# Batch sizes, output loads and the order of the last groups in a graph layer's sum over edges

## The chip, the core and the metric

The kernel runs on one core of a Trainium2 chip. The time is device microseconds (us) of one execution, the median of several; before the change it is 1443.45 us (three runs, 1440.51 to 1446.14). A core has TensorE (PE, matmuls; its weight loads are listed as PEld), VectorE (DVE), ScalarE (ACT), GpSimd (POOL), and SyncE (SP), which issues plain DMAs. POOL issues the indirect DMAs, the gathers.

## What is computed

One layer of a graph network on 12,500 nodes of 128 features, with 200,000 edges sorted by destination and four edge types. Cut to what matters:

```python
h = jnp.maximum(_layernorm(x, axis=-1), 0.0)
xs = h[src]
for i in range(4):
    msgs = msgs + jnp.where((edge_type == i)[:, None], xs @ W[i] + b[i], 0.0)
out = x + jax.ops.segment_sum(msgs, dst, num_segments=N)
```

Destinations are drawn as the square of a uniform number, so low node numbers get far more edges than high ones.

## The kernel before

Edges are cut into 1563 chunks of 128. The normalised features are kept in a table `htab` in HBM as three bf16 parts of each number (384 columns a node). There are two ways to sum the edges of a node.

*Gathered chunks.* The 1083 chunks from number 480 on are taken in groups of 16 (66 full groups, then groups of 12, 8, 4 and 3). For a chunk, `gather` (L440) fetches 128 rows of the table with one indirect DMA into half of a group's tile `hm`; a tile holds 8 chunks and there are five such tiles. VectorE makes a one-hot matrix `oh` from the destination and type of each edge (L461), TensorE multiplies the gathered rows by it (L498, three matmuls a chunk, one for each part), ScalarE copies the sums `ps` to `sb` (L505), TensorE applies the bias (L510) and the four weight matrices (L512) into `py`, and VectorE adds 16 windows of `py` into a ring buffer at rows that it reads from `brow` (`add_up`, L515 and L524). The first eight groups ("raw") gather `x` itself and normalise it, since the table is still being built. Raw groups put their additions on a list `waiting`, which the next group empties.

When the ring has a node block that no later chunk reaches, `put_out` and `leave` write it: load the rows of `x` into `xo` (L538), transpose the sums on TensorE (L546), add on VectorE (L549), store (L551, L553). A list `flushes` holds the blocks, with a due chunk for each (L577), and `goes` names the group after which each is written; what is not due among the full groups leaves after the last group.

*Counted nodes.* The first 480 chunks go to 1224 destinations with many edges each. For those the kernel counts how often each table row and type occurs. `count` takes a batch of nodes: for each slot (up to 128 edges of a node) VectorE makes two one-hot matrices `o` (L782 or L786, and L787), TensorE multiplies them (L791), and ScalarE copies the result to `counts` as 8-bit numbers (L794), two nodes in one 16-bit number where they can share. The two `o` tiles hold four slots each. `multiply` then reads the whole table once for a batch, 25 loads `hs` of up to 384 KB (L823, five buffers), with three matmuls for each of 98 table blocks (L826, 294 in all), whose moving columns are four times the batch's nodes; then a product with the weights (L841) and additions into `acc`. `dense_work` runs the multiplication of one batch beside the counting of the next.

There are 1260 entries (a node with very many edges has several), in batches of 22, 46, twelve of 92, 42 and 46. The first two take only nodes that share a slot; later ones mix in nodes that have several slots.

What sets the order: Python emits the work of a group, and `pace` says how far the dense work should be after each part of a group, counted in matmul columns; from the last full group on, all that is left is emitted. The blocks `tc.issue_after(mm)` tie the emitted work to a matmul; the framework then orders each engine's instructions. The engines run them in that order and wait for one another by semaphores. SP's loads stand in one queue, POOL's gathers in another.

```python
ends_in = [12, 8, 4, 3]
sizes = [G] * FULL + ([r] if r else []) + ends_in
```

`check_all` (L591) checks the ring's ranges and the counts, and sets a flag; the program's last part runs a slow version if the flag is set.

Of the kernel before, what the change touches and what calls it, by code (L numbers as in the profile page):

```python
# [48 lines left out]
P = 128  # L49
# [3 lines left out]
SG = 4  # L53
WIN = 32
RAW = 8
ROOM = 12
C0 = 480
VBMAX = 92
MANY = 16
# [3 lines left out]
OT = 4  # L63
# [6 lines left out]
def kernel(  # L70
# [56 lines left out]
    shared = [(0, d) for d in range(PAIRS, ND)]  # L127

    VB = VBMAX
    sizes_of = [VB // 8 * 2, VB // 4 * 2]  # L130
    left = len(alone) + len(shared) - sum(sizes_of) - VB // 4 * 2
    sizes_of += [VB] * (left // VB) + ([left % VB] if left % VB else []) + [VB // 4 * 2]
    batches = []
    a = b0 = 0
    for i, n in enumerate(sizes_of):

        na, ns = len(alone) - a, len(shared) - b0
        n1 = 0 if i < 2 else min(round(n * na / (na + ns) / 2) * 2, na)
        n1 = max(n1, n - ns)
        batches.append(alone[a : a + n1] + shared[b0 : b0 + n - n1])  # L140
        a, b0 = a + n1, b0 + n - n1
# [309 lines left out]
    def sum_up(t0, g, rows, raw, last):  # L451
        win = window_of(C0 + t0)
        K = NT * win
        if raw:
            oh = npool.tile([P, G, P], F32, name="ohf")[:, :, :K]
        else:
            while waiting:
                waiting.pop()()
            oh = opool.tile([P, G, P], BF16, name="oh")[:, :, :K]
        for i in range(g):  # L460
            nc.vector.tensor_scalar(  # L461
                oh[:, i, :], (iota_f if raw else iota_b)[:, :K], keyf[:, t0 + i : t0 + i + 1], None, ALU.is_equal
            )
        if raw:
            for h0 in range(0, g, HG):
                row = lambda k: rows(h0 + k, 0, 1)
                n = min(HG, g - h0)
                of = stats(row, n, P, npool, "")
                normalize(row, row, n, P, of)

            with tc.issue_after(of[2]):
                while waiting:
                    waiting.pop()()
        sb = spool.tile([P, G * P], F32, name="sb")[:, : G * K].rearrange("p (g t n) -> p g t n", g=G, t=NT)
        def types():

            ohv = oh.rearrange("p g (t n) -> p g t n", t=NT)
            pc = s_ps.tile([R, G * WIN], F32, name="ps")[:, : G * win].rearrange("p (g n) -> p g n", g=G)
            for t in range(NT):
                if raw:  # L480
                    nc.tensor.matmul(pc[:, :g, :], pick_f[:, t, :], ohv[:, :g, t, :], start=(t == 0), stop=(t == NT - 1))  # L481
                else:
                    nc.tensor.matmul(  # L483
                        pc[t * CG : (t + 1) * CG, :g, :], three, ohv[:, :g, t, :], start=True, stop=True, tile_position=(0, t * CG)
                    )
            cnt = spool.tile([R, G * WIN], BF16, name="cnt")[:, : G * win].rearrange("p (g n) -> p g n", g=G)
            nc.scalar.copy(cnt[:, :g], pc[:, :g])  # L487
            return cnt

        R = N3 if raw else P  # L490
        cnt = None if raw else types()
        nparts = 1 if raw else 3
        for i0 in range(0, g, SG):
            i1 = min(i0 + SG, g)
            ps = s_ps.tile([P, SG, P], F32, name="ps")[:, :, :K]
            for i in range(i0, i1):
                for c in range(nparts):
                    mm = nc.tensor.matmul(  # L498
                        ps[:, i - i0, :],
                        rows(i, c, nparts),  # L500
                        oh[:, i, :],
                        start=(c == 0),
                        stop=(c == nparts - 1),
                    )
            nc.scalar.copy(sb[:, i0:i1].rearrange("p g t n -> p g (t n)"), ps[:, : i1 - i0, :])  # L505
            yield i1 / g, mm.ins
        if raw:
            cnt = types()
        py = (x_ps.tile([P, G * WIN], F32, name="pt") if last else y_ps.tile([P, G * WIN], F32, name="py"))[:, : G * win].rearrange("p (g n) -> p g n", g=G)
        nc.tensor.matmul(py[:, :g, :], b12 if raw else b128, cnt[:, :g, :], start=True, stop=False)  # L510
        for t in range(NT):
            mm = nc.tensor.matmul(py[:, :g, :], wsb[:, t, :], sb[:, :g, t, :], start=False, stop=(t == NT - 1))  # L512

        def add_up():
            _, at = nc.values_load_multi_w_load_instructions(  # L515
                brow[0:1, t0 : t0 + g],
                engines=[DVE],
                min_val=0,
                max_val=RING - 1,
                skip_runtime_bounds_check_because="the row is clamped to this range on the chip",  # L520
            )
            for i in range(g):
                to = ring[:, bass.ds(at[i], win)]
                nc.vector.tensor_tensor(to, to, py[:, i, :], ALU.add)  # L524

        if raw:
            waiting.append(add_up)
        else:
            add_up()
        yield 1, mm.ins  # L530


    def leave(j0, j1, of, c0):

        nf = min(j1, N // P) - j0
        xt = outp.tile([P, OT, D], F32, name="xo")
        if nf:
            nc.sync.dma_start(xt[:, :nf, :], x[j0 * P : (j0 + nf) * P, :].rearrange("(j p) d -> p j d", p=P))  # L538
        if j0 + nf < j1:
            r = rows_of(j1 - 1)  # L540
            nc.sync.dma_start(xt[:r, nf, :], x[(j1 - 1) * P :, :])
        pt = x_ps.tile([P, OT, DO], F32, name="pt")
        for j in range(j0, j1):
            r = rows_of(j)
            k = c0 + (j - j0) * P
            nc.tensor.transpose(pt[:r, j - j0, :], of[:, k : k + r], ident)  # L546
        for r, a0, a1 in ((P, 0, nf), (rows_of(j1 - 1), nf, j1 - j0)):
            if a1 > a0:
                nc.vector.tensor_add(xt[:r, a0:a1, :], pt[:r, a0:a1, :], xt[:r, a0:a1, :])  # L549
        if nf:  # L550
            nc.sync.dma_start(out[j0 * P : (j0 + nf) * P, :].rearrange("(j p) d -> p j d", p=P), xt[:, :nf, :])  # L551
        if j0 + nf < j1:
            nc.sync.dma_start(out[(j1 - 1) * P :, :], xt[: rows_of(j1 - 1), nf, :])  # L553
# [18 lines left out]
    while flushes[-1][1] < NW:  # L572
# [1 line left out]
        jb = min(ja + OT, NW, (ja * P // RING + 1) * RING // P)  # L574
        flushes.append((ja, jb, 0))
    assert NDT * P <= RING - 512
    flushes = [(ja, jb, T * (min(jb * P, N) / N) ** 0.5 + ROOM - C0) for ja, jb, _ in flushes]  # L577


    ends_in = [12, 8, 4, 3]  # L580
# [2 lines left out]
    sizes = [G] * FULL + ([r] if r else []) + ends_in  # L583
    starts = [sum(sizes[:i]) for i in range(len(sizes))]

    goes = [
        next((i for i in range(RAW, FULL) if starts[i] + sizes[i] >= c), len(sizes) - 1) for _, _, c in flushes
    ]


    def check_all():  # L591

        low = const.tile([P, BM], F32, name="low")
        step = const.tile([P, BM], F32, name="step")
# [1 line left out]
        for (ja, jb, _), i in zip(flushes, goes):  # L596
            if starts[i] + sizes[i] < TM:
# [1 line left out]
                    step, rowf, starts[i] + sizes[i] - 0.5, (jb - ja) * float(P), ALU.is_gt, ALU.mult  # L599
                )  # L600
                nc.vector.tensor_add(low, low, step)
        bad = const.tile([P, 5], F32, name="bad")
        hi = const.tile([P, 4], F32, name="hi")
        nc.vector.tensor_sub(low, head, low)
        nc.vector.tensor_reduce(hi[:, 0:1], ends[:, :, 0], AX.X, ALU.max)
# [3 lines left out]
        nc.vector.tensor_single_scalar(bad[:, 0:1], hi[:, 0:1], -0.5, op=ALU.is_gt)  # L609
        nc.vector.tensor_single_scalar(bad[:, 1:3], hi[:, 1:3], -0.5, op=ALU.is_lt)  # L610
        nc.vector.tensor_single_scalar(bad[:, 3:4], hi[:, 3:4], RING - WIN + 0.5, op=ALU.is_gt)
        nc.vector.tensor_single_scalar(bad[:, 4:5], most, MANY + 0.5, op=ALU.is_gt)
        many = const.tile([P, 3], F32, name="many")
        nc.vector.tensor_reduce(many[:, 0:1], bad, AX.X, ALU.add)
# [301 lines left out]
    for gi, (t0, g) in enumerate(zip(starts, sizes)):  # L916
# [71 lines left out]
                prep_edges(q, q + 1, later, 1)  # L988
        if gi == RAW - 1:
            assert done >= len(tables)  # L990
        for part, mm in sum_up(t0, g, rows, raw, gi >= FULL):

            with tc.issue_after(mm):
                while work and spent < pace(gi, part):
                    spent = next(work, None)
                    if spent is None:
                        work = None
        if gi in SLOT_STEPS:
            with tc.issue_after(mm):
                for _ in range(SLOT_STEPS[gi]):  # L1000
                    next(to_slots, None)
        if gi == RAW - 1:
# [4 lines left out]
            whats.close()  # L1007
            outp = mid.enter_context(tc.tile_pool(name="outp", bufs=3))
            later = mid.enter_context(tc.tile_pool(name="later", bufs=1))
            dense = mid.enter_context(tc.tile_pool(name="dense", bufs=2))  # L1010
            sdp = mid.enter_context(tc.tile_pool(name="sdp", bufs=1))
            ohp = mid.enter_context(tc.tile_pool(name="ohp", bufs=2))
            hsp = mid.enter_context(tc.tile_pool(name="hsp", bufs=5))
            work = dense_work()
        for (ja, jb, _), i in zip(flushes, goes):
            if i == gi:
                put_out(ja, jb, t0 + g < TM)
        if work is None and not dense_out and gi > RAW:
            dense_out = True
            assert goes[0] < gi  # L1020
            for ja in range(0, NDT, OT):
                leave(ja, min(ja + OT, NDT), acc, ja * P)
        if dense_out and not checked:
            checked = True
            check_all()
# [126 lines left out]
```

## Time and profile before

| what | value |
|---|---|
| median of three runs | 1443.45 us |
| the profiled execution's own time | 1440.69 us |
| its span, first to last instruction | 1439.0 us |
| mean granted TensorE clock | 0.937 |
| raw groups, table building and slots | about 0 to 219 us |
| first gather from `htab` to the end of the last | 177.2 to 1414.9 us |
| matmuls of L826 | 4704, 715.7 us busy |
| HBM traffic of all DMAs | 290.10 MB |

In the profile's rows "out<-in" are the program's tile names. A mean of one instruction is from its start to its end; matmuls overlap, so the step from one to the next is shorter than that. In brackets stands how long the engine was idle before an instruction and what ended the idle time. The chain of waits follows the work that ended last back in time. "Built order" below means the order of instructions on each engine in the compiled program, which holds no times.

### The profile page before, as it was taken

The numbers are of one execution on the slowest core, as the hardware profiler recorded it, in microseconds if no ns is written. First come the engines' busy times: TensorE is split into PE (matmuls) and PEld (weight loads), VectorE is DVE, ScalarE is ACT, GpSimd is POOL, SyncE is SP. The second block draws the span as 40 slices with busy tenths as digits, with TensorE's granted clock in tenths as the row PEclk, the third lists the DMA queues.
The fourth block names the chain that finished last, engine by engine and source line by source line (L and its number), as shares of the span: only waits on it lengthen the run. The fifth ranks groups of instructions, "written<-read, shape, count | busy, mean of one in ns | idle before, by whom it ended". The sixth has DMA issues, their size and how long they took to land.

```text
span 1439.0 us, 31409 instructions
## 1 busy us (share of the span) xinstructions
PE 1274.2 (89%) x10210; PEld 857.0 (60%) x10210; DVE 982.2 (68%) x5310; ACT 598.0 (42%) x1922; POOL 1059.0 (74%) x1093
## 2 busy tenths in 40 slices
PE   0656687989999899999999997899999999999975
PEld 0434455765666566666656664566666666668763
DVE  8698696888888667657575765586676766557323
ACT  7776445352343535243343534244343535233220
POOL 7777777575777777777777777777777777777772
PEclk9765678999999999999999998899999999999997
DMA  6543247965666576776667674667667676768952
GB/s 210 176 153 104 93 150 255 312 214 168 201 197 201 173 238 193 233 221 203 212 200 221 208 223 139 193 203 216 210 206 223 195 210 206 220 207 288 324 184 82
DMA packets 144633, 290.10 MB, mean 202 GB/s; under 512 B 27116, under 2 KB 74654, under 8 KB 144462
## 3 DMA queue, kind: packets, MB, share of 16 engines
q1 hardware_dynamic: 94526, 185.71, 39.9%
q0 software_dynamic: 49936, 102.34, 24.7%
q8 instruction: 80, 1.31, 0.4%
q14 instruction: 91, 0.75, 0.2%
HBM read 271.91 MB, written 16.03 MB: 200 GB/s over the span
## 4 chain that ended last, share of the span: by engine, by line
PE 67%; DVE 8%; DMA 6%; POOL 6%; issue 3%; ACT 3%; DVEq 0%; SPq 0%; ACTq 0%; POOLq 0%
PE pa L826 36%; PE pt L791 10%; PE py L512 8%; PE ps L498 7%; POOL hm L440 6%; DMA hs<-htab 3%; ACT counts L794 2%; DVE ring L524 2%; DVE o L787 2%; DMA hm<-htab,srcT 1%; DVE o L786 1%; DVE oh L461 1%; PE ps L481 1%; PE py L841 1%; PE ps L483 1%
## 5 line engine op out<-in xcount | busy, mean ns | idle before, releaser
L440 POOL DMA_INDIRECT hm<-htab,srcT x955 | 925.2, 969 | 313.5 <-issue 267.5
L826 PE MATMUL pa<-counts,hs 128*128 128x368 fp8e4 (+3 forms) x4704 | 715.7, 298 | 14.4 <-DMA hs<-htab 13.1
L826 PEld LDWEIGHTS <-hs 128*128 128x128 bf16 x4704 | 427.8, 98 | 239.1 <-DMA hs<-htab 20.2
L794 ACT ACTIVATE counts<-pt 128x392 uint16<-128x392 f32 x630 | 309.4, 504 | 279.1 <-PE pt L791 275.7
L787 DVE TENSOR_SCALAR o<-iota_n,hkT 128x392 bf16<-128x392 f16 x1083 | 359.5, 332 | 0.0
L791 PE MATMUL pt<-o,o 128*128 128x392 bf16 x1083 | 278.9, 334 | 6.6 <-ACT counts L794 2.5
L524 DVE TENSOR_TENSOR ring<-ring,py 128x16 f32 (+4 forms) x1056 | 182.2, 173 | 124.3 <-PE py L512 104.0
L461 DVE TENSOR_SCALAR oh<-iota_b,keyT 128x64 bf16<-128x64 bf16 (+4 forms) x955 | 174.0, 264 | 107.3 <-PE ps L498 106.6
L505 ACT COPY sb<-ps 128x256 f32<-128x256 f32 (+5 forms) x271 | 111.8, 417 | 311.8 <-PE ps L498 276.7
L498 PE MATMUL ps<-oh,hm 128*128 128x64 bf16 (+4 forms) x2865 | 154.3, 202 | 29.5 <-DMA hm<-htab,srcT 29.1
L498 PEld LDWEIGHTS <-hm 128*128 128x128 bf16 x2865 | 131.5, 99 | 64.2 <-DMA hm<-htab,srcT 36.0
L512 PE MATMUL py<-sb,wsb 128*128 128x384 f32 (+4 forms) x528 | 164.5, 452 | 0.0
L440 POOL DMA_INDIRECT hm<-in_x_dram,srcT x128 | 132.3, 1033 | 41.8 <-issue 36.0
L782 DVE TENSOR_SCALAR o<-iota_b,loT 128x128 bf16<-128x128 bf16 x375 | 99.1, 264 | 88.5 <-PE pt L791 87.8
L786 DVE TENSOR_SCALAR o<-iota_b,loT,byT 128x128 bf16<-128x128 bf16 x333 | 110.9, 333 | 40.6 <-PE pt L791 40.1
L791 PEld LDWEIGHTS <-o 128*128 128x128 bf16 x1083 | 100.4, 99 | 56.3 <-DVE o L787 10.9
L794 ACT ACTIVATION_READ_ACCUMULATOR counts<-pt 128x1 f32 x630 | 131.9, 209 | 0.0
L512 PEld LDWEIGHTS py<-sb,wsb 128*128 128x128 f32 x528 | 105.8, 211 | 35.2 <-issue 9.9
L498 PE MATMUL ps<-ohf,hm 128*128 128x48 f32 x256 | 59.1, 385 | 52.9 <-ACT hm L402 52.9
L487 ACT CAST cnt<-ps 128x256 bf16<-128x256 f32 (+7 forms) x70 | 28.6, 409 | 165.5 <-PE ps L483 144.9
L786 DVE TENSOR_SCALAR o<-iota_b,loT 128x128 bf16<-128x128 bf16 x375 | 95.9, 256 | 1.3 <-PE pt L791 1.2
L498 PEld LDWEIGHTS ps<-ohf,hm 128*128 128x128 f32 x256 | 52.1, 291 | 71.7 <-ACT hm L402 59.1
(188 smaller groups left out, 641.9 us busy)
## 6 DMA issues: line engine op xcount, KB each, us to landing
hs<-htab SPq DMA_DIRECT2D x384, 384.0 KB
hm<-htab,srcT POOLq DMA_INDIRECT x955
htab<-h SPq DMA_DIRECT2D x11, 768.0 KB
xo<-in_x_dram SPq DMA_DIRECT2D x23, 256.0 KB
out_dram<-xo SPq DMA_DIRECT2D x23, 256.0 KB
xt<-in_x_dram SPq DMA_DIRECT2D x6, 512.0 KB
hs<-htab SPq DMA_DIRECT2D x16, 192.0 KB
xt<-in_x_dram SPq DMA_DIRECT2D x5, 448.0 KB
```

Of the source, the lines that this page charges most:

```text
L440: nc.gpsimd.indirect_dma_start(out=rows[:, (i - h0) * width : (i - h0 + 1) * width], out_offset=None, in_=table, in_offset=bass.IndirectOf ...
L461: nc.vector.tensor_scalar(oh[:, i, :], (iota_f if raw else iota_b)[:, :K], keyf[:, t0 + i : t0 + i + 1], None, ALU.is_equal)
L498: mm = nc.tensor.matmul(ps[:, i - i0, :], rows(i, c, nparts), oh[:, i, :], start=(c == 0), stop=(c == nparts - 1),)
L505: nc.scalar.copy(sb[:, i0:i1].rearrange("p g t n -> p g (t n)"), ps[:, : i1 - i0, :])
L512: mm = nc.tensor.matmul(py[:, :g, :], wsb[:, t, :], sb[:, :g, t, :], start=False, stop=(t == NT - 1))
L524: nc.vector.tensor_tensor(to, to, py[:, i, :], ALU.add)
L782: nc.vector.tensor_scalar(o1[:, k, :], iota_b, loT[:, s : s + 1], None, ALU.is_equal)
L786: nc.vector.tensor_scalar(o1[:, k, :], iota_b, loT[:, s : s + 1], by, ALU.is_equal, ALU.mult)
L787: nc.vector.tensor_scalar(o2[:, k, :], iota_n, hkT[:, s : s + 1], None, ALU.is_equal)
L791: nc.tensor.matmul(pb, o1[:, k, :], o2[:, k, :], start=first, stop=last)
L794: nc.scalar.activation(counts[:, :, i * NT : (i + 1) * NT], pb.rearrange("p (b t) -> p b t", t=NT), AF.Copy, accum_out=both[:, i : i + 1],)
L826: nc.tensor.matmul(pa[:, : nv * NT], hs[:, j - j0, c * D : (c + 1) * D], counts[:, j, : nv * NT], start=(j == 0 and c == 0), stop=(j == NW ...
```

## The change

There are five edits.

1. Batches: the batch that isn't full (1260 entries less 13 x 92, so 64) comes first, and all others have 92, so that 14 batches are left of 16. Only the first takes shared nodes alone.
2. Counting buffers are given back once the dense work is done. In their room a pool `outs` holds all outputs that are still to come, and their rows of `x` are loaded there at once (`fetch`); `leave` uses them.
3. Due times: the margin is no longer 12 chunks but 2 plus 6 standard deviations of the number of edges, in chunks. A block may now leave after the last group but one. Three of the 24 blocks leave one group earlier by this, among them the last but one (from node 92 x 128 on), which leaves after the group of 4.
4. In the small groups at the end, all of a group's instructions are tied to the matmuls of the group before it (`behind`), so that matmuls stand in group order. The last group's additions wait until the block that leaves ahead of it has been written.
5. `check_all` is split: the range checks run at group 63.

```diff
-ROOM = 12
+ROOM = 6
...
-    sizes_of = [VB // 8 * 2, VB // 4 * 2]
-    left = len(alone) + len(shared) - sum(sizes_of) - VB // 4 * 2
-    sizes_of += [VB] * (left // VB) + ([left % VB] if left % VB else []) + [VB // 4 * 2]
+    left = len(alone) + len(shared)
+    sizes_of = ([left % VB] if left % VB else []) + [VB] * (left // VB)
...
-        n1 = 0 if i < 2 else min(round(n * na / (na + ns) / 2) * 2, na)
+        n1 = 0 if i < 1 else min(round(n * na / (na + ns) / 2) * 2, na)
...
-        if raw:
+        if raw or t0 + g == TM:
             waiting.append(add_up)
...
+    def due(jb):
+
+        q = (min(jb * P, N) / N) ** 0.5
+        return T * q + 2 + ROOM * (q * (1 - q) * E) ** 0.5 / P - C0
...
+        next((i for i in [*range(RAW, FULL), final - 1] if starts[i] + sizes[i] >= c), final) for _, _, c in flushes
...
+        behind = ExitStack()
+        if gi >= FULL:
+            behind.enter_context(tc.issue_after(mm))
         for part, mm in sum_up(t0, g, rows, raw, gi >= FULL):
...
+        behind.close()
...
+            counting.close()
+            leaves = [(ja, min(ja + OT, NDT)) for ja in range(0, NDT, OT)]
+            late = [(ja, jb) for (ja, jb, _), i in zip(flushes, goes) if i >= gi]
+            outp = mid.enter_context(tc.tile_pool(name="outs", bufs=len(leaves + late)))
+            for ja, jb in leaves + late:
+                seen_out[ja] = fetch(ja, jb)
+            for ja, jb in leaves:
+                leave(ja, jb, acc, ja * P)
+        for (ja, jb, _), i in zip(flushes, goes):
+            if i == gi < final - 1:
+                put_out(ja, jb, True)
+        if gi == final:
+
+            for ahead in (True, False):
+                for (ja, jb, _), i in zip(flushes, goes):
+                    if i >= final - 1 and (i < final) == ahead:
+                        put_out(ja, jb, False)
+                while waiting:
+                    waiting.pop()()
+        if gi == FULL - 3:
+            assert q == BM - 1
+            check_chunks()
```

`fetch` is the part of `leave` that loads `x`, made a function of its own.

More of the change, by code (lines that the diff above doesn't have):

```diff
@@ L530, in sum_up, with fetch @@
         yield 1, mm.ins
-    def leave(j0, j1, of, c0):
+    seen_out = {}
+    def fetch(j0, j1):
         nf = min(j1, N // P) - j0
@@ L541, in leave @@
             nc.sync.dma_start(xt[:r, nf, :], x[(j1 - 1) * P :, :])
+        return xt
+    def leave(j0, j1, of, c0):
+        nf = min(j1, N // P) - j0
+        xt = seen_out.pop(j0) if j0 in seen_out else fetch(j0, j1)
         pt = x_ps.tile([P, OT, DO], F32, name="pt")
@@ L576 @@
     assert NDT * P <= RING - 512
-    flushes = [(ja, jb, T * (min(jb * P, N) / N) ** 0.5 + ROOM - C0) for ja, jb, _ in flushes]
+    def due(jb):
+        q = (min(jb * P, N) / N) ** 0.5
+        return T * q + 2 + ROOM * (q * (1 - q) * E) ** 0.5 / P - C0
+    flushes = [(ja, jb, due(jb)) for ja, jb, _ in flushes]
     ends_in = [12, 8, 4, 3]
@@ L584, with check_chunks @@
     starts = [sum(sizes[:i]) for i in range(len(sizes))]
+    final = len(sizes) - 1
     goes = [
-        next((i for i in range(RAW, FULL) if starts[i] + sizes[i] >= c), len(sizes) - 1) for _, _, c in flushes
+        next((i for i in [*range(RAW, FULL), final - 1] if starts[i] + sizes[i] >= c), final) for _, _, c in flushes
     ]
-    def check_all():
+    bad = const.tile([P, 5], F32, name="bad")
+    def check_chunks():
         low = const.tile([P, BM], F32, name="low")
@@ L601, in check_all @@
                 nc.vector.tensor_add(low, low, step)
-        bad = const.tile([P, 5], F32, name="bad")
         hi = const.tile([P, 4], F32, name="hi")
@@ L611, in check_all @@
         nc.vector.tensor_single_scalar(bad[:, 3:4], hi[:, 3:4], RING - WIN + 0.5, op=ALU.is_gt)
+    def check_all():
         nc.vector.tensor_single_scalar(bad[:, 4:5], most, MANY + 0.5, op=ALU.is_gt)
@@ L1009 @@
             later = mid.enter_context(tc.tile_pool(name="later", bufs=1))
[L1010 to L1013, printed above, removed]
+            counting = mid.enter_context(ExitStack())
+            dense = counting.enter_context(tc.tile_pool(name="dense", bufs=2))
+            sdp = counting.enter_context(tc.tile_pool(name="sdp", bufs=1))
+            ohp = counting.enter_context(tc.tile_pool(name="ohp", bufs=2))
+            hsp = counting.enter_context(tc.tile_pool(name="hsp", bufs=5))
             work = dense_work()
-        for (ja, jb, _), i in zip(flushes, goes):
-            if i == gi:
-                put_out(ja, jb, t0 + g < TM)
         if work is None and not dense_out and gi > RAW:
@@ L1020 @@
             assert goes[0] < gi
-            for ja in range(0, NDT, OT):
-                leave(ja, min(ja + OT, NDT), acc, ja * P)
+            counting.close()
[19 more added lines that the diff above has]
+            check_chunks()
         if dense_out and not checked:
```

## The prediction

> **What bounds the kernel now.** The page comes first, because its shares mislead here: TensorE looks like the limit.
>
> ```profile
> span 1439.0 us, 31409 instructions
> PE 1274.2 (89%) x10210; PEld 857.0 (60%) x10210; DVE 982.2 (68%) x5310; ACT 598.0 (42%) x1922; POOL 1059.0 (74%) x1093
> L440 POOL DMA_INDIRECT hm<-htab,srcT x955 | 925.2, 969 | 313.5 <-issue 267.5
> ```
>
> The POOL row says otherwise. One gather takes 969 ns and 0.30 us passes before the next, so 955 of them need 955 x 1.27 = 1212 us if nothing stops them. The gathers run from 177.2 to 1414.9, which is 1237.6 us. So POOL is stopped for only about 24 us; all the rest is back to back. POOL's timeline, filtered to the long gaps, shows where:
>
> ```profile
> 280.08 0.94 POOL L440 DMA_INDIRECT hm<-htab,srcT  x1 [10.85 <-PE ps L498]
> 332.32 0.94 POOL L440 DMA_INDIRECT hm<-htab,srcT  x1 [8.72 <-PE ps L498]
> ```
>
> Five tiles hm of 8 gathers each exist, so POOL waits there for the matmuls of L498 five tiles earlier. From 332 to 1414.9 there are only two more gaps (2.2 and 0.6 us, at 966 and 987). **The time is therefore: start of gathers (177.2) + 1212 + 24 of stops + what follows the last gather (1414.9 to 1439.0, 24.1 us).** A change helps only through the stops, through slower gathers, or behind the last one.
>
> Why is TensorE late at 280? Its chain of waits in 219 to 345 names the table loads:
>
> ```profile
> 231.74 6.59 DMA hs<-htab
> 239.06 6.34 DMA hs<-htab
> 245.44 0.65 PE pa L826 x12
> 246.12 5.52 DMA hs<-htab
> 255.24 7.04 DMA hs<-htab
> ```
>
> The first batch has 22 nodes. Its 12 matmuls per load take about half a microsecond, while a 384 KB load arrives every 1.2 us: the batch is bound by DMA (share 0.84, 291 GB/s in 219.5 to 262). Between 219.5 and 280, 41 us of matmul steps take 60.
>
> **The change, part by part.** *Batches.* Sixteen batches (22, 46, twelve of 92, 42, 46) become fourteen (64 and thirteen of 92); nodes, columns and the 1083 counted slots stay. Two passes over the table go: 2 x 294 matmuls, 50 loads, 19 MB of 290. What are 588 small matmuls worth? By the rows, from first start to last end, less one matmul's own length:
>
> ```profile
> 249.49 0.65 PE L826 MATMUL pa<-counts,hs 128*128 128x88 fp8e4 x12 [0.54 <-DMA hs<-htab]
> 1299.81 1.90 PE L826 MATMUL pa<-counts,hs 128*128 128x168 fp8e4 x24
> 260.39 1.11 PE L826 MATMUL pa<-counts,hs 128*128 128x184 fp8e4 x12
> 499.70 1.41 PE L826 MATMUL pa<-counts,hs 128*128 128x368 fp8e4 x8
> ```
>
> (0.65-0.21)/11 = 40 ns for 88 columns, 72 for 168, 79 for 184, 156 for 368: 0.42 ns a column and no fixed part. For 256 columns I estimate 109. Before: 294 x (40+79+72+79) = 79.4 us; after: 294 x (109+156) = 77.9. Two fewer closing products (16 steps of L841 at 0.11) make 1.8. TensorE gains 3 us in all. The Trainium skill speaks otherwise ("TensorE: Matmul & The Clock Gate", Back-to-back issue gap): a weight load with each matmul keeps its spacing at about 81 ns for 128 columns and 131 for 512. Worked through as a straight line that would give 294 x (338 - 210 ns) = 38 us. The rows of this very matmul decide: 3 us, and off the path besides.
>
> *What the first batch does to the stops.* Up to tile 8 (0-based; its release ended the stop at 332) the built orders hold the same TensorE work (79.8 us before, 78.7 after, from the first gathered matmul at 219.5) and the same slots (161, 162). The mix differs: after, 32 slots are counted before the first table matmul. Such a slot costs ScalarE 0.47 us (copies at 221.44, 221.91, 222.38) and VectorE 0.23+0.22 us, against 0.17 on TensorE. So TensorE is at its first table matmul at about 220.5 + 32 x 0.47 + 1.7 (copies of group 8) = 237. From there each load serves 12 matmuls of 109 ns and 4 to 5 slots, 2.1 us; loads can come every 1.2, so the DMA waits (7.4 us on PE's own row, some 10 with the weight loads) should go. Release of tile 4: 237 + 33 us of matmuls = 270; VectorE's line is the same: it is 8 slots ahead at 237 (two buffers of four), so 57 further slots x 0.40, two groups' one-hots 4.6, ring adds 2.4, acc and xo 3.5, from 237, give 270. POOL needs it at 269.2 to run on (before: 279.9). Tile 8: 237 + 70 = 307 by TensorE, 309 with a second run of 23 slots; needed at about 311. So the sums just meet the need. In before they missed it by 19 to 24 us, 10 of that DMA waits. What is left (engines waiting for one another, half clock at 327 to 332) was 9 to 12 us; I leave **8 us** of stop, bounds 0 (the sums hold) and 19.3 (as before). Gain here 19.3 - 8 = **11**. After 332 TensorE's step per tile is 9.2 to 9.6 us against POOL's 10.1, so it falls back no more; what is late next is POOL itself.
>
> *Later stops.* Before, the built order does tiles 64 to 68 almost empty and then 46 us of work in one piece before tile 69; that is the 2.2 + 0.6 at 966 and 987. After, those tiles carry 7 to 13 us each. Gain **2.3** (the 0.3 of each gap stays). The biggest piece left (36 us, tile 43) was 34 before and had 9 us of room.
>
> *Slow gathers.* What gathers take over the usual 0.945 us adds up to 22 us, 8.6 of it between 250 and 450, when loads are densest. A pass less there: **1.5** gained, bounds 0 and 4.
>
> *The tail.* Before, the L510/L512 products of groups 66 to 68 stand behind the output transposes, and the additions come late, one group after the other:
>
> ```profile
> 1421.68 0.42 DVE L549 TENSOR_TENSOR xo<-pt,xo 128x256 f32<-128x256 f32 x1 [1.25 <-DMA xo<-in_x_dram]
> 1424.64 1.72 DVE L524 TENSOR_TENSOR ring<-ring,pt 128x28 f32 x8 [0.69 <-DVE ring L524]
> 1426.80 0.83 DVE L524 TENSOR_TENSOR ring<-ring,pt 128x28 f32 x4 [0.44 <-DVE ring L524]
> 1428.49 0.62 DVE L524 TENSOR_TENSOR ring<-ring,pt 128x28 f32 x3 [0.86 <-DVE ring L524]
> ```
>
> After, groups 66, 67 and 68 (18.8, 8.8 and 3.8 us before the last gather's end) finish while POOL gathers. Behind the last gather stay: landing 1.7 (gather at 1410.19, its matmul at 1412.86), three matmuls 0.35, copy 0.5, product 1.2, three transposes and xo 1.4, index load and three additions 1.4, two transposes 0.7, two additions 0.5, and from the last addition to the span's end 7.5 as now (1431.5 to 1439.0): 15.3. A rule speaks against the order: the Trainium skill ("TensorE: Matmul & The Clock Gate", What's actually happening) has the array fall to half clock when it idles, and group order makes it idle for each gather. The row: clock 0.65 in 1395 to 1406, and eight products took 4.61 us at 1405.8 against 3.17 at 1388.3. On 2 us of TensorE work that is 0.9 by the row, 2 by the rule; I take 0.9. Tail 16.2, gain **8**. The x loads ahead remove the wait of 1.25 (3.9 us of DMA in the chain), already in this sum. Their price: seven loads need the counts' memory, so SP holds them until the last batch is done, and VectorE's additions of the first output, with the ring additions behind them, wait some 6 us for the landing (hs row). Cover: the last batch ends some 28 us before the last gather does, and POOL then has 20 us of room. The chunk checks, brought forward, are short VectorE work of 0.1 us each, covered by VectorE's idle third.
>
> Sum: 11 + 2.3 + 1.5 + 8 = 22.8 off 1439.0, span 1416. The profiled execution took 1440.69 (1.7 more than its span) and lies 2.8 under the median of 1443.45: **1421** as a median.
>
> **Rivals.** *The early stops stay* (the count run of 32 slots costs what the DMA waits cost): speaks for it that tiles 2 and 3 get 29 and 47 more slots ahead of them, and have 3 and 11 us of room; against, that the total by tile 8 is equal. Only later stops and tail: 1443.45 - 11 = 1432. *It does nothing*: POOL runs ahead, TensorE does not follow and the gain is given back at the end: 1442. *Slower:* the same, and the last batch ends less than 12 us before the last gather. Then x loads (6 us), first output, and four groups in strict order, each with copy, product and index load, line up behind it: about 33 us behind the gather instead of 24: 1452. Against it: TensorE had caught up with the gathers at 1394. *All stops go*: 1443.45 - 32 = 1411, within the first case.
>
> **Numbers.** Likeliest case 0.69 (1421, itself 1407 to 1432), early stops stay 0.18 (1432), nothing 0.08 (1442), slower 0.05 (1452). The 80% range 1407 to 1436 takes in stops of 0 and 19 and a tail 4 us worse. A measurement tells 0.5% (7 us) from no change; faster needs under 1436.2, which the first case nearly always and the second mostly gives: 0.82; same 0.13; slower 0.05.
>
> **What would show it.** Right: no DMA hs wait in 230 to 262; POOL's gaps at tiles 8 to 13 summing to under 12 us; last gather ending near 1400; TensorE's busy time lower by some 3 us alone; 16 us from the last gather to the end. Wrong: a gap at 258 or 269 of over 10 us behind L498, new gaps after 340, or xo waiting for its load near the end.

## The result and the profile after

The changed kernel takes 1428.89 us (median of five runs, 1425.77 to 1432.76) beside 1443.59 for the kernel before on the same chip (five runs): ratio 0.9902, 95% interval 0.9876 to 0.9927. It is 1.0% faster, by 14.7 us, where 22 were forecast. The profiled execution took 1428.53 us. Lines behind the change have moved: the gather is L439, the edge matmul L497, the table matmul L843, the slot's matmul L808 and its copy L811.

The page of the changed kernel:

```profile
span 1426.7 us, 30085 instructions
PE 1281.1 (90%) x9606; PEld 840.1 (59%) x9606; DVE 978.9 (69%) x5293; ACT 594.9 (42%) x1920; POOL 1055.2 (74%) x1093
L439 POOL DMA_INDIRECT hm<-htab,srcT x955 | 922.1, 966 | 314.3 <-issue 269.6
```

There are 604 matmuls fewer, yet PE's busy time is no lower (1281 us, 1274 before). POOL still sets the time: its gathers, back to back but for a few gaps, fill the span from 176.9 to 1412.3 us. Its long gaps from 255 to 340 us:

```profile
263.12 0.94 POOL L439 DMA_INDIRECT hm<-htab,srcT  x1 [11.47 <-PE ps L497]
333.06 0.94 POOL L439 DMA_INDIRECT hm<-htab,srcT  x1 [8.13 <-PE pt L808]
```

These are the two early stops that were to shrink to 8 us together. The first has moved 17 us ahead and is 0.6 us longer; the second is where it was and 0.6 us shorter. Their sum is 19.6 us in both kernels. After 340 us there is none. Behind the last gather the chain of work is short:

```profile
1411.36 2.91 DMA hm<-htab,srcT
1414.27 0.05 issue
1414.32 0.48 PE ps L497 x3
...
1414.87 0.45 ACT sb L504
1415.32 0.04 issue
1415.36 2.00 PE pt L511 x8
1417.37 0.65 PE pt L553 x3
1418.02 0.02 issue
1418.04 0.69 DVE xo L556
...
1419.78 0.68 PE pt L553 x2
1420.45 0.02 issue
1420.48 0.30 DVE xo L556
```

Landing, three matmuls, copy, product, transposes and output, three ring additions (among the rows left out), transposes and the last output at 1420.96: no work of groups 66 to 68 stands in between, and up to there no DMA other than the gather itself. In the kernel before, the same chain held a store and a load of `xo`:

```profile
1415.51 2.19 DMA out_dram<-xo
1417.71 3.88 DMA xo<-in_x_dram
```

and then 7.3 us of ring additions with their index loads (1421.79 to 1429.12).

The span, split in the terms of the forecast. "Stops" are what POOL's gaps of over 0.5 us between gathers have beyond the usual 0.29 us, before and after gather 200; "slow gathers" is what gathers take beyond 0.945 us; "tail" is the end of the last gather to the end of the span. The last four rows are experiments of the next section.

| kernel | first gather | last ends | early stops | later stops | slow gathers | tail | span | ratio to before |
|---|---|---|---|---|---|---|---|---|
| before | 177.2 | 1414.9 | 19.6 | 2.3 | 22.5 | 24.1 | 1439.0 | 1 |
| after | 176.9 | 1412.3 | 22.7 | 0 | 19.3 | 14.4 | 1426.7 | 0.9902 (0.9876 to 0.9927) |
| batches alone | 178.9 | 1415.7 | 22.5 | 0 | 20.9 | 26.3 | 1442.0 | 0.9962 (0.9942 to 0.9981) |
| old batches | 176.8 | 1415.3 | 20.6 | 1.4 | 23.1 | 14.6 | 1429.9 | 0.9902 (0.9876 to 0.9928) |
| six tiles | 181.3 | 1406.6 | 10.2 | 0 | 21.5 | 14.4 | 1421.0 | 0.9809 (0.9780 to 0.9838) |
| late pace | 177.5 | 1399.7 | 3.7 | 0 | 25.0 | 14.4 | 1414.0 | 0.9757 (0.9728 to 0.9787) |

From before to after: start -0.3, early stops +3.1, later stops -2.3, slow gathers -3.2, tail -9.7, together -12.4; the spans differ by 12.3.

The +3.1 of the early stops does not lie in the two stops above. It lies ahead of them, where a gather waits for a tile of the raw groups:

```profile
210.73 0.94 POOL L439 DMA_INDIRECT hm<-htab,srcT  x1 [3.42 <-PE ps L497]
```

This gap is 0.9 us before, 1.8 with the batches alone, and 3.4 in old batches and late pace too. PE itself is later there: its first matmul on gathered table rows comes at 222.2 in place of 219.8. Why is not known.

### The profile page after: what moved, and what is told of

It is laid out like the page before. It is cut to its first block, busy times and chain, and to the rows that moved or that the text cites. A ratio compares the mean times of both kernels' runs of the same rounds, so it can differ in the third digit from the quotient of the medians.

```text
span 1426.7 us, 30085 instructions
## 1 busy us (share of the span) xinstructions
PE 1281.1 (90%) x9606; PEld 840.1 (59%) x9606; DVE 978.9 (69%) x5293; ACT 594.9 (42%) x1920; POOL 1055.2 (74%) x1093
## 2 busy tenths in 40 slices
DMA packets 137427, 270.75 MB, mean 190 GB/s; under 512 B 26316, under 2 KB 73598, under 8 KB 137262
## 3 DMA queue, kind: packets, MB, share of 16 engines
q8 instruction: 76, 1.25, 0.3%
## 4 chain that ended last, share of the span: by engine, by line
PE 69%; DVE 7%; POOL 7%; issue 4%; ACT 3%; DMA 2%; DVEq 0%; POOLq 0%; ACTq 0%
PE pa L843 37%; PE pt L808 10%; PE ps L497 8%; PE py L511 8%; POOL hm L439 7%; DMA hm<-htab,srcT 2%; ACT counts L811 2%; DVE o L804 2%; PE ps L480 1%; PE py L858 1%; DVE ring L523 1%; PE ps L482 1%; DVE o L803 1%; DVE oh L460 1%; DVE st L382 1%
## 5 line engine op out<-in xcount | busy, mean ns | idle before, releaser
L439 POOL DMA_INDIRECT hm<-htab,srcT x955 | 922.1, 966 | 314.3 <-issue 269.6
L843 PE MATMUL pa<-counts,hs 128*128 128x368 fp8e4 (+1 forms) x4116 | 708.2, 318 | 0.0
L843 PEld LDWEIGHTS <-hs 128*128 128x128 bf16 x4116 | 401.5, 99 | 229.5 <-issue 6.5
L811 ACT ACTIVATE counts<-pt 128x392 uint16<-128x392 f32 x630 | 309.0, 506 | 228.9 <-PE pt L808 227.0
L808 PE MATMUL pt<-o,o 128*128 128x392 bf16 x1083 | 274.5, 336 | 6.5 <-ACT counts L811 4.7
L497 PE MATMUL ps<-oh,hm 128*128 128x64 bf16 (+4 forms) x2865 | 156.8, 203 | 26.1 <-DMA hm<-htab,srcT 25.9
L497 PEld LDWEIGHTS <-hm 128*128 128x128 bf16 x2865 | 133.8, 99 | 64.1 <-DMA hm<-htab,srcT 32.3
L439 POOL DMA_INDIRECT hm<-in_x_dram,srcT x128 | 131.6, 1028 | 42.1 <-issue 35.0
L808 PEld LDWEIGHTS <-o 128*128 128x128 bf16 x1083 | 99.9, 99 | 66.7 <-DVE o L804 12.7
L811 ACT ACTIVATION_READ_ACCUMULATOR counts<-pt 128x1 f32 x630 | 133.6, 212 | 0.0
L497 PE MATMUL ps<-ohf,hm 128*128 128x48 f32 x256 | 59.8, 391 | 51.3 <-ACT hm L401 51.3
L497 PEld LDWEIGHTS ps<-ohf,hm 128*128 128x128 f32 x256 | 53.1, 298 | 70.5 <-ACT hm L401 57.1
## 6 DMA issues: line engine op xcount, KB each, us to landing
xo<-in_x_dram SPq DMA_DIRECT2D x23, 256.0 KB
out_dram<-xo SPq DMA_DIRECT2D x23, 256.0 KB
```

What stands on the lines that cost most here:

```text
L439: nc.gpsimd.indirect_dma_start(out=rows[:, (i - h0) * width : (i - h0 + 1) * width], out_offset=None, in_=table, in_offset=bass.IndirectOf ...
L497: mm = nc.tensor.matmul(ps[:, i - i0, :], rows(i, c, nparts), oh[:, i, :], start=(c == 0), stop=(c == nparts - 1),)
L808: nc.tensor.matmul(pb, o1[:, k, :], o2[:, k, :], start=first, stop=last)
L811: nc.scalar.activation(counts[:, :, i * NT : (i + 1) * NT], pb.rearrange("p (b t) -> p b t", t=NT), AF.Copy, accum_out=both[:, i : i + 1],)
L843: nc.tensor.matmul(pa[:, : nv * NT], hs[:, j - j0, c * D : (c + 1) * D], counts[:, j, : nv * NT], start=(j == 0 and c == 0), stop=(j == NW ...
```

## Where the early stops come from

Three views of the changed kernel tell why there is a stop at tile 2 (0-based), the tile whose release ended the first one. First the timeline of one stretch in the run of 32 slots that now comes before any table matmul:

```profile
232.10 0.50 ACT L811 ACTIVATE counts<-pt 128x392 uint16<-128x392 f32 x1
232.26 0.33 PE L808 MATMUL pt<-o,o 128*128 128x392 bf16 x1 [0.15 <-ACT counts L811]
232.47 0.21 ACT L811 ACTIVATION_READ_ACCUMULATOR counts<-pt 128x1 f32 x1
232.57 0.51 ACT L811 ACTIVATE counts<-pt 128x392 uint16<-128x392 f32 x1
232.74 0.33 PE L808 MATMUL pt<-o,o 128*128 128x392 bf16 x1 [0.15 <-ACT counts L811]
```

ScalarE's copies start 0.47 us apart, and PE's matmuls follow at 0.48, though one step of PE is 0.166 us (392 columns). PE loses 0.31 us with each slot. VectorE's two one-hots a slot take 0.46 us here as well (232.33 to 232.79), so two engines hold the run. The chain of waits shows the run, and then what comes next:

```profile
227.90 11.48 ACT counts L811 x48
...
251.96 1.48 DVE acc L567
253.43 0.61 DVE xo L556
254.04 0.20 issue
254.25 1.12 DVE ring L571
255.43 0.48 DVE ring L571
256.00 0.35 PE ps L482 x4
```

L567, L556 and L571 are the first output: in VectorE's queue its additions and the clearing of the ring stand before the last one-hot of the group whose matmuls would release the tile. PE's waits from 219.5 to 262:

```profile
PE ps L482 <- DVE oh L460: 3.3, 1, 3.3
PE pt L808 <- ACT counts L811: 2.8, 14, 0.8
PE pt L553 <- DVE oh L460: 2.1, 1, 2.1
```

and PE's clock behind it (the number ahead of the last two is the granted clock):

```profile
249.60:256.00 6.40, 0.96 (x8) 0.52 (x6) 6.09 (x26) 0.45 (x2) 1.75 (x2) 0.85 0.63 211
256.00:261.00 5.00, 5.00 (x34) 3.22 (x34) 3.08 (x16) 1.22 (x4) 0.00 (x0) 0.51 0.23 60
```

PE works 0.96 us of 6.4, and then runs the next 5 us at 0.51 of its clock. The Trainium skill ("TensorE: Matmul & The Clock Gate", What's actually happening) has the array at half clock after an idle window of about 3.4 us; the trace agrees with it here. The forecast cited it for the tail only.

So tile 2 is free at 263.0, where POOL wanted it at 251.6. The forecast's way of counting, from the first table matmul at 237 and each later matmul at its full-clock step, puts its release near 251. Of the 12 us between, the trace gives 2.7 to the later first table matmul (239.73, not 237), 5.8 to PE's two waits for VectorE (from one start to the next, 249.6 to 252.03 and 252.39 to 256.0, less the step of the matmul that starts there; the rows record 2.1 and 3.3), and some 2.5 to half clock (12 table matmuls in 2.56 us that take 1.31 at full clock, and nearly as much for the slots and edge matmuls beside them). The rest, 1 us, is not assigned.

This explains the stop's place, but not the sum of both stops. The second stop ended with the release of tile 8 in both kernels, at 332.1 before and 332.8 after, the tile that the gathers of tile 13 go into. PE waits for no gather on the way there, so without the first stop the second would have been longer by as much. So the question is why PE took as long as before to tile 8. Two stretches from the first matmul on gathered table rows to that release, before and after, each with PE's longest waits in it (the clock is again ahead of the last two numbers):

```profile
219.80:332.10 112.30, 95.16 (x1081) 70.23 (x1078) 92.00 (x497) 49.96 (x189) 71.93 (x71) 0.97 0.75 252
PE pa L826 <- DMA hs<-htab: 7.4, 13, 1.4
PE ps L483 <- DVE oh L461: 6.0, 2, 4.0
```

```profile
222.20:332.80 110.60, 98.47 (x792) 66.38 (x788) 92.24 (x487) 48.36 (x185) 70.26 (x71) 0.89 0.57 172
PE pt L808 <- ACT counts L811: 4.0, 22, 0.8
PE ps L482 <- DVE oh L460: 3.3, 1, 3.3
```

The work is the same, as forecast. All recorded waits of PE fall from 16.0 to 11.5 us, but the clock falls from 0.97 to 0.89. An estimate from PE's timelines (each step from one start to the next, less 0.42 ns a column, f32 columns counted twice) shares out what PE lost: 34 us before and 32 after. Loads 10 and then none; slot copies on ScalarE 3 and then 8; low clock 4 and then 12; VectorE about 9 in both; the rest, small steps that no row explains, 7 and then 3. So waits for VectorE's queue are not new with the change. Slot copies and low clock took the place of the loads.

## Experiments

Theory: the early stops are a debt. The plan asks for more work of the first groups than the engines give in the time that five tiles of gathers cover; the cover has a fixed size, and which wait runs it down matters little. Rivals: single waits that come from the order in the queues and not from the amount of work; and that the batches, not the end of the program, gained the time.

**Batches alone**: the kernel before with only this.

```diff
-    sizes_of = [VB // 8 * 2, VB // 4 * 2]
-    left = len(alone) + len(shared) - sum(sizes_of) - VB // 4 * 2
-    sizes_of += [VB] * (left // VB) + ([left % VB] if left % VB else []) + [VB // 4 * 2]
+    left = len(alone) + len(shared)
+    sizes_of = ([left % VB] if left % VB else []) + [VB] * (left // VB)
...
-        n1 = 0 if i < 2 else min(round(n * na / (na + ns) / 2) * 2, na)
+        n1 = 0 if i < 1 else min(round(n * na / (na + ns) / 2) * 2, na)
```

> The kernel before with the new batch sizes and nothing else of the change (64, then thirteen of 92). My theory now: the changed kernel's two early stops of GpSimd (11.5 and 8.1 us) belong to the new batches, as those of before (10.9 and 8.7 us) did to the old ones, and most of the gain of the change came from behind the last gather. Then this kernel keeps both early stops (sum 18 to 24 us), loses the two later ones (2.9 us), ends its last gather at 1411 to 1414 us and keeps a tail of about 24 us behind it: span 1434 to 1438, time about 1438 to 1441. Rival, that the batches are what gained most and the tail little: time 1430 to 1433.

Measured: 1441.66 us beside 1446.79 for before (this and the next three share a chip and its runs of before). Early stops 22.5, later stops none, tail 26.3, with gaps in the places of the changed kernel:

```profile
266.16 0.95 POOL L439 DMA_INDIRECT hm<-htab,srcT  x1 [13.31 <-PE ps L497]
336.29 0.94 POOL L439 DMA_INDIRECT hm<-htab,srcT  x1 [8.28 <-PE pt L790]
```

The stops belong to the batches, and the batches alone are worth 0.2 to 0.6%. The profiled run's span lies outside the 1434 to 1438 expected, and the time is 0.7 us above its range: the profiled run had a gap of 5.7 us ahead of the first table gather (1.4 before) and a tail 2 us longer than before's.

**Old batches**: the changed kernel with the two hunks above turned back, so only the edits at the end are new.

> The changed kernel with the old batch sizes (22, 46, twelve of 92, 42, 46), so only the edits at the end of the program are new. My theory: the stops are those of before (10.9, 8.7, 2.2 and 0.6 us), the last gather ends at about 1415 us, the waits of PE on the rows that SP loads for the counts (7.4 us between 219 and 345 us) are back, and the tail behind the last gather is 14 to 16 us: time 1432 to 1436. Rival, that the tail gains only with the new batches, which leave PE more room at the end: the tail is 20 us or more and the time 1439 or more.

Measured: 1432.12 us. The stops of before are back at their places (the kernel's gather line is L440):

```profile
281.57 0.94 POOL L440 DMA_INDIRECT hm<-htab,srcT  x1 [9.11 <-PE ps L498]
333.84 0.94 POOL L440 DMA_INDIRECT hm<-htab,srcT  x1 [8.50 <-PE ps L498]
```

The tail is 14.6 us, and PE waits for loaded rows again (5.5 us between 219 and 345; 7.4 before, none in the changed kernel). Two different first batches, with different waits, stop POOL for 20.6 and 22.7 us. The edits at the end give the whole gain within the interval; the rival that they need the new batches falls. On top of them the new batches add nothing that the intervals show.

**Six tiles** of gathered rows, the room taken from other buffers.

```diff
-    hpool = mid.enter_context(tc.tile_pool(name="rows", bufs=5))
+    hpool = mid.enter_context(tc.tile_pool(name="rows", bufs=6))
...
-        xt = npool.tile([P, XG, D], F32, name="xt", bufs=4)
+        xt = npool.tile([P, XG, D], F32, name="xt", bufs=3)
...
-            hsp = counting.enter_context(tc.tile_pool(name="hsp", bufs=5))
+            hsp = counting.enter_context(tc.tile_pool(name="hsp", bufs=3))
```

> The changed kernel with six tiles of gathered rows in place of five; the room for it comes from the rows that SP loads for the counts (three buffers in place of five) and from a node buffer of the first stage (three in place of four). My theory, that the early stops are a debt of PE against a cover of five tiles of gathers: a sixth tile gives about 10 us more cover once (8 gathers of 1.25 us), the two stops shrink from 19.6 us together to 8 to 11 us, the last gather ends at 1402 to 1404 us and the time is about 1419, as long as three buffers for the loaded rows bring no new wait of PE. Rival, that the stops come from single waits of PE that grow with the cover, or that the three buffers stall PE: no change, or slower by up to 5 us.

Measured: 1420.08 us.

```profile
267.45 0.94 POOL L439 DMA_INDIRECT hm<-htab,srcT  x1 [3.81 <-PE ps L497]
336.83 0.94 POOL L439 DMA_INDIRECT hm<-htab,srcT  x1 [6.98 <-PE pt L808]
```

The early stops fall from 22.7 to 10.2 us, but 3.6 of these 12.5 us are the gaps at the raw groups, which the sixth tile closes. The two stops shown fall from 19.6 to 10.8 us, 8.8 less for eight gathers of 1.25 us more cover. The extra cover counts once over both stops, not at each, so the rival of waits that grow with the cover falls. Whether PE is late by work or by waits, this run can't tell: either way one more tile covers 10 us. The last gather ends 3 us later than expected because the first table gather starts 4.4 us later, behind a wait of 5.6 us for the table's last store; the node buffer given up is the likely reason, but it was not tried alone.

**Late pace**: the same work, planned later.

```diff
+LAG = 0.03
...
-        return ((n + part) * a_group - sum(own[:n]) - part * own[n]) / dense_columns()
+        on = ((n + part) * a_group - sum(own[:n]) - part * own[n]) / dense_columns()
+        return on - LAG * (1.0 - on)
```

> The changed kernel with the pace of the dense work (counts and table matmuls) set back by 0.03 of its total at the start, and caught up evenly to the end. My theory: the early stops are too much dense work among the first groups for the cover, while from 400 us on PE has 24 to 38 us to spare. So the stops of 11.5 and 8.1 us fall under 3 us in sum, the last gather ends at 1393 to 1397 us, the tail stays at 14 to 16 us, time 1409 to 1414. Rival, that the first counts on ScalarE and VectorE hold the groups however few come at a time (one long wait, not a debt): stops only come later, and the time stays at 1426 to 1431.

Measured: 1412.8 us, the fastest kernel of the study. With a window from 205 us to the last gather, one row of POOL's timeline has a gap of over 1 us:

```profile
211.91 0.94 POOL L440 DMA_INDIRECT hm<-htab,srcT  x1 [3.44 <-PE ps L498]
```

It waits for a tile of the raw groups, which the pace does not reach. Tile 2 is released at 231.3 in place of 263.0, and no tile is late by the end; the smallest room after 300 us is 4 us (tile 44). Both stops are gone, though the 32 slots still come before the first table matmul (252.56). But the order is not as it was. The first output now stands behind the matmuls of tiles 2 and 3 and not ahead of them, as these rows of PE and VectorE show:

```profile
230.29 1.58 PE L498 MATMUL ps<-oh,hm 128*128 128x48 bf16 x48
234.46 1.55 DVE L568 TENSOR_TENSOR acc<-acc,ring 128x1280 f32<-128x1280 f32 x1
```

So this run changes the amount and the order together, and the rival of single waits is weakened, not refuted. The sizes speak for the amount. Tile 8 is released at 300.7, 32 us earlier; up to there PE has 46 slots and 114 table matmuls fewer than in the changed kernel, some 22 us by their steps (an estimate). The wait ahead of tile 2 that the new order avoids, with the low clock behind it, was 5.8 + 2.5 us. And the clock is lower still here, 0.74 in 219 to 262 us beside 0.83 in the changed kernel, without a stop: a wait or a low clock matters only while a tile is late. A run with the old amount in the new order is missing. The last gather ends at 1399.7, not 1393 to 1397: slow gathers took 25.0 us, 5.7 more than in the changed kernel, and the stop of 3.4 us is left. Why gathers were slower is not known.

**A true price for the slots, and the parts of the end.** Eight further runs of six kernels were meant to tell how much of the debt is the price of a slot in the plan, and which edit carries the tail.

```diff
+PRICE = 2.9
...
-        return NSLOTS * float(NB) + sum(len(vs) for vs in batches) * NW * 3.0 * NT
+        first = sum(len(slots_of(u)) for u in units(batches[0])) * (PRICE - 1.0)
+        return (NSLOTS + first) * float(NB) + sum(len(vs) for vs in batches) * NW * 3.0 * NT
...
-                steps[count(*now)] = sum(len(slots_of(u)) for u in units(vs)) * a_slot
+                steps[count(*now)] = sum(len(slots_of(u)) for u in units(vs)) * a_slot * (PRICE if vs is batches[0] else 1.0)
```

> The changed kernel, whose plan of the dense work prices a slot of counts of the first batch at 2.9 times its TensorE columns: 0.48 us, the spacing that the trace shows while slots are counted alone, in place of 0.166. All later slots keep their price. My theory: the stops stayed because the plan takes the run of 32 slots for 5 us of work and it takes 15; with the true price about 10 us of dense work leave the first groups, the stops fall from 22.7 us in sum to 10 to 14, the last gather ends at 1401 to 1405 us, time 1417 to 1422. Rival, that the stops come from the order in the queues of VectorE and ScalarE, whatever the amount: stops 20 us or more, time 1426 to 1431.

Without the group order of the small groups:

```diff
-        if gi >= FULL:
-            behind.enter_context(tc.issue_after(mm))
```

> The changed kernel without the group order of the small groups at the end: their products need not follow the matmuls of the group before them. Nothing ahead of 1370 us changes, so the last gather ends at 1411 to 1414 us. My theory, that this order is what let groups 66 to 68 finish while POOL still gathers: the tail behind the last gather grows from 14.4 us to 18 to 24, time 1432 to 1438. Rival, that PE's and the additions' order at the end come from the other edits: the tail stays at 14 to 15.5 us, time 1426 to 1431.

Without the loads of x ahead:

```diff
-            for ja, jb in leaves + late:
-                seen_out[ja] = fetch(ja, jb)
```

> The changed kernel with x for an output loaded when the output is made, not ahead in the counts' room. My theory: in the kernel before the wait for this load was 1.25 us of a longer chain, and here the chain behind the last gather is shorter (the last addition before the output is 4.5 us behind the gather's end), so the load's 2.5 us of transfer, issued late, is more open: tail 15.5 to 18 us, time 1428 to 1433. Rival, that SP issues it early enough anyway: tail 14.4 us as now, same time.

With the old due rule:

```diff
-        return T * q + 2 + ROOM * (q * (1 - q) * E) ** 0.5 / P - C0
+        return T * q + 12 - C0
```

> The changed kernel with the old rule for when a finished piece of the ring goes out. My theory: with the old rule one or two pieces more go out behind the last gather, or VectorE and PE have them in one lump ahead of it; each piece costs PE some 1.4 us and VectorE 0.5 us there: tail 15 to 19 us, time 1428 to 1434. Rival, that the rule moves pieces only in the middle, where nothing waits for them: tail 14.4 us, time within 2 us of the changed kernel's.

True price and no order again (e9, e10), then without loads ahead and with the old due rule (e11), then true price without the group order (e12):

> The kernel of e5 again, because the chip of e5 to e8 ran the kernel before at 2060 us and tells nothing of stops at 1440. As for e5: by my theory (the plan takes the run of 32 slots for 5 us of work and it takes 15) the stops fall from 22.7 us in sum to 10 to 14, the last gather ends at 1401 to 1405 us, time 1417 to 1422. By the rival (order in the queues of VectorE and ScalarE, whatever the amount) stops stay at 20 us or more, time 1426 to 1431.

> The kernel of e6 again on another chip. My theory, that the group order of the small groups is most of the gain behind the last gather: that tail grows from 14.4 us to 18 to 24, time 1432 to 1438. Rival, that the other edits carry it: tail 14 to 15.5 us, time 1426 to 1431.

> The changed kernel without the x loads ahead and with the old due rule for pieces of the ring, so that of the edits at the end the group order and the order of the last additions stay. My theory: the tail is 14.4 to 17 us, because the load and the pieces lie mostly beside other work, time 1427 to 1432. Rival, that x loaded ahead or the due rule carry the tail: 18 us or more, time 1432 or more.

> Two edits that are read in two places of the profile, because the chips of e5 to e11 ran the kernel before at 2060 us or more: the slots of the first batch priced at 2.9 times their columns in the plan (read ahead of 340 us), and the small groups at the end without group order (read behind the last gather). On the price, my theory (the plan takes the run of 32 slots for 5 us and it takes 15): the stops fall from 22.7 us in sum to 10 to 14 and the last gather ends at 1401 to 1405 us; rival (queue order, whatever the amount): stops of 20 us or more. On the order, my theory (it carries most of the gain behind the last gather): the tail is 18 to 24 us in place of 14.4; rival (the other edits carry it): 14 to 15.5 us. Time 1421 to 1428 if I am right on both.

All eight ran on chips where the kernel before takes 2058 to 2084 us, and there they answer neither question. Times, with the ratio to before on the same chip:

| kernel | time, us | ratio | early stops | later stops | tail |
|---|---|---|---|---|---|
| true price (e5) | 1983.58 | 0.962 (0.958 to 0.966) | 126.6 | 369.9 | 31.0 |
| no order (e6) | 1944.71 | 0.944 (0.940 to 0.948) | 116.4 | 342.2 | 33.5 |
| no loads ahead (e7) | 1938.77 | 0.942 (0.938 to 0.946) | 115.3 | 334.5 | 32.0 |
| old due rule (e8) | 1962.48 | 0.952 (0.948 to 0.956) | 133.6 | 349.2 | 30.6 |
| true price again (e9) | 2023.29 | 0.969 (0.963 to 0.975) | 128.4 | 408.8 | 33.5 |
| no order again (e10) | 1987.77 | 0.953 (0.948 to 0.957) | 135.9 | 364.7 | 32.8 |
| order alone (e11) | 1994.02 | 0.958 (0.953 to 0.963) | 129.7 | 368.8 | 31.9 |
| price and no order (e12) | 1980.83 | 0.961 (0.957 to 0.965) | 120.7 | 375.8 | 32.8 |

Here POOL is stopped for 450 to 540 us and PE is late all the way; a tail of 30.6 to 33.5 us is PE finishing, and the same kernel's tail differs by 2.5 us between two runs (e5, e9), as one kernel's ratio does (no order, 0.944 and 0.953). So differences of 1 to 3 us between the edits at the end can't be read, and the price of a slot is not tried under the conditions that it was meant for. What stays open: how the 9.7 us of the tail divide among order, loads ahead and due rule, and whether the price of the slots alone would remove half the stops. One thing does show: true price is slower than its neighbours on both chips where it ran beside them (by 21 to 45 us on the first, 29 and 36 on the second). That dense work put off is not caught up where PE has no room would explain it, and would hold for the late pace too; neither is shown.

## Why the forecast came out as it did

*POOL's gathers bound the kernel*: right. With 955 x 1.25 us for the gathers and their usual gaps the table's parts add up to each span within 0.5 us, and with the stops gone the time falls by nearly as much (late pace: stops -19.0, slow gathers +5.7, span -12.7).

*TensorE's saving of 3 us by fewer passes is off the path*: right as to the path; the 3 us can't be seen in the busy time, which rose by 7 us. The matmul rate of 0.42 ns a column held: 12 matmuls of 256 columns take 1.31 us in the chain at 261.08, 109 ns each, as estimated from the four other widths.

*Loads no longer hold PE*: right, 7.4 us to none. *Early stops, 11 us gained*: wrong; -3.1. This is the step that failed, and it is most of the miss. The two stops gained nothing (19.6 us in both kernels), and the gap at the raw groups, which the forecast did not have, holds the 3.1. The forecast summed TensorE's and VectorE's work up to tiles 4 and 8, where the kernel before had its stops, and left 8 us for engines waiting for one another and for half clock. The work was counted right; the 8 us is the term that failed. Tile 8 was to be released at 307 to 309, and was at 332.8. The run of slots was in the forecast's sum (32 slots at 0.47 us in place of 0.17, some 10 us); what was left to the 8 us came to some 23 by the estimate above: low clock 12, VectorE 9, and a start 2 us later. The loads went, as forecast, but the low clock and the slot copies that came with the new batch cost as much. The first stop moved to tile 2, whose 3.0 us of room stood in the trace and which gets 29 more slots ahead of it, as the forecast itself said under its first rival. To sum that tile as well would not have shown it, for the same reason: by the forecast's count it is free at 251, just when POOL wants it. The rival *the early stops stay* (1432; its two terms make 10.3, so 1433) describes what happened, and its reason, that the count run costs what the loads cost, fits the losses up to tile 8. The forecast's own sign of being wrong came too, a gap of over 10 us behind the matmuls of gathered rows: 11.5 us, at 263 in place of 258 or 269.

*Later stops, 2.3*: right, to the tenth. *Slow gathers, 1.5*: 3.2 in this pair of traces, but 19 to 25 us over six traces of this study without a pattern, so it is not shown that the change caused it.

*Tail, 8*: 9.7. By its parts: landing 2.0 (forecast 1.7), matmuls and copy 1.0 (0.85), product 2.0 at low clock (2.1), transposes and first output 1.4 (1.4), index load and additions 0.9 (1.4), transposes and last output 1.3 (1.2), from the last addition to the end 5.7 where 7.5 was taken over from before. The low clock's price, 0.9 us by the row and 2 by the rule, came near the row's. The wait for x is gone, as said.

*The slower case* (x loads late at the end) did not come: the last batch's closing product ends at 1365, 47 us before the last gather, and PE is 23 to 39 us ahead of the gathers' need after 900 us.

The sum, from 22.8: early stops 14.1 short, tail 1.7, slow gathers 1.7 and start 0.3 over, gives 12.4 of span. The median moved by 14.6 from the 1443.45 forecast from; the spread of the runs is 7 us. That the time lies inside the forecast's range (1407 to 1436) is owed to its width, to a tail and gathers 3.4 us better than their terms, and to 2.3 us between profiled executions and medians. The largest term did not come true, so this is in part luck.

## What to carry to other kernels

Where a fast producer runs over a ring of a few tiles, the last late tile sets the sum of the stops, and an earlier stop only takes its share in advance. So ask what the engine loses up to that tile, in waits and in clock, and not only which wait goes: here another took its place. If a plan spreads side work evenly and there is room later, plan less of it at the start: that gave 13 us of span here, while other contents of the early work alone gave 3 to 8 us and nothing that shows on top of the edits at the end.

## What the runs showed of the chip besides

On the chips of the last eight runs single instructions last as long as elsewhere (in e6 966 ns for a gather and 507 for a slot copy; 966 and 506 in the changed kernel), but engines stand still in waits that the trace puts down to "remote", not to an engine or a DMA of this core. In the last run (e12), ScalarE's and PE's timelines near 700 us:

```profile
692.21 0.19 ACT L812 ACTIVATION_READ_ACCUMULATOR counts<-pt 128x1 f32 x1
710.72 0.50 ACT L812 ACTIVATE counts<-pt 128x392 uint16<-128x392 f32 x1 [18.31 <-remote]
```

```profile
711.36 5.74 PE L809 MATMUL pt<-o,o 128*128 128x392 bf16 x12 [18.41 <-ACT counts L812]
```

After 330 us, PE has 51 steps of more than 2 us there, 204 us in sum; in the changed kernel 5, 14 us in sum. The moved bytes are the same (270.75 MB), over a longer span. The record gives chip number 4 both for e1 to e4, where the kernel before took 1446.79 us, and for e12, where it took 2058.13, so the number does not tell the two apart. What stops the engines is not known.
